# A four-layer transformer block in fp32: last token tiles reordered, one adapter product in another PSUM bank, last loads moved

## The chip, the cores and the metric

The kernel runs on one core of one Trainium2 chip. The metric is device time in microseconds of one execution of the whole program; the time before is the median of three runs. One more execution was taken with the profiler, and its trace is what the prediction reads. PE is TensorE (matmuls; PEld its weight loads), DVE is VectorE, ACT is ScalarE, POOL is GpSimd, SP is SyncE, which here issues most DMAs.

## The reference

Four stages, each followed by a residual sum and a layernorm without weights, on x of 4 batches x 1024 tokens x 1024 features, all in fp32:

```
x = layernorm(x + x @ (W0 * blockmask).T)                       # stage 0
x = layernorm(x + x @ W1.T + bias1 + lora(batch))               # stage 1: an adapter of rank 16 picked by batch
x = layernorm(x + convnet(x))                                   # 4 layers of width 128: norm, silu, long convolution, norm, MLP 512
x = layernorm(x + x @ W3.T + bias3 + sum_e routing_e lora_e(x)) # stage 3: 8 adapters of rank 16, routed by the batch's mean
```

## The kernel before, in words

**Tiles and stages.** Tokens go in eight groups of 512 (`g` = 0 to 7; a batch is two groups). Stages 0 and 1 keep features on the partitions; each is 14 products per group (a Strassen-like scheme of 7 products for 8 blocks, in two halves of the output columns, `project`, L429). Stage 3 has the tokens on the partitions: a group is two tiles of 2 x 128 tokens (`stage3(g, i, ...)`, L673), and each tile takes 7 products, k = 0 to 6, of four matmul steps with 512 columns. An fp32 matmul step is two instructions in the trace, so a product is 8 MATMULs of 512 columns, or 16 of 256 in stages 0 and 1.

**The order of the work.** One product of the main chain is one *tick*. A dictionary `plan` holds small pieces of other work by tick: `put(at, piece)` and `put_in(lo, hi, pieces, ...)` put them there, `later(n, piece)` puts one n ticks from now, and `tick()` (L373) runs what stands at the present tick and counts on. PE and DVE execute strictly in the order in which the program names their instructions (class `InOrder`: every operation of `V` and `T` is made to follow the one before, and is recorded at L104). The queues of ACT, POOL and SP are ordered by the compiler, which may issue a load as soon as its buffer is free. Ticks 28g to 28g+13 are stage 0 of group g, the 14 after them stage 1; ticks from 224 are stage 3.

**PSUM.** `bank()` gives one of four banks of 128 x 512 in the pool "mm", for the main products. `spot()` gives one of two in the pool "pc", used by `cv` (convolution result), `a_ps` (first matmul of the MLP), `aTp` (transposes of an adapter) and, in the start, two of the first products. A bank comes free when the last reader of its product (a DVE addition or an ACT copy) is done.

**Adapters.** `merge` (L731) adds an adapter to a weight matrix: for every 128 rows it multiplies two small matrices (48 rows deep in stage 1, 128 in stage 3) and DVE adds the product to the weight (`w<-w,mm`), in column halves j = 0, 1. With 48 rows the two halves lie at partitions 0 and 64 of `aT` and `b`, so the two products of a pair stand in different rows of the array. `adapt1(b)` does this for stage 1 of batch b, in 8 pieces of two products; after every second piece, `operands` makes four sums and stores the result for streaming. For batch 0 the pieces stand between the last half products of stage 0 of group 0 (`for o in range(5, KC)`, L1263); for batches 1 to 3 they are put at ticks 56b-1 to 56b+9. At tick 56b+8 three pieces and `into` (L549, the product `mm<-z,win`) come together.

**The last adapter and bias.** `last_prep` (tick 68) runs the three steps of `prep_lora(a3_d, b3_d, ...)` (L1029): load `at_raw` and `b_raw` through SP, eight transposes on PE into two spots `aTp`, copies and centring on ACT and DVE and three stores on POOL; and the same for the bias row `b3r`.

**The end of a stage 3 tile.** Rows are normed by the root of their mean square: `squares(m, n)` (ACT, with a running sum into `st`) for the column halves n of the token tiles m = 0, 1; then `spread4(m)` (a small DVE operation, a root on ACT) and `finish(m)` (reciprocal and scaling of 128 x 1024 on DVE, a store of 512 KB on SP). Product k = 5 finishes token tile 0 and k = 6 finishes token tile 1. Both `spread4` stand one tick after the tile's last product, `finish(0)` and `finish(1)` one and two ticks later still; behind the very last tile there are no products left, so they run one after the other.

Of the kernel before, what the change touches and what calls it, by code (L numbers as in the profile page):

```python
# [10 lines left out]
F32 = mybir.dt.float32  # L11
I32 = mybir.dt.int32
AF = mybir.ActivationFunctionType
ALU = mybir.AluOpType
# [3 lines left out]
P = 128  # L18
NB = 4
S = 1024  # L20
D = 1024
# [3 lines left out]
HF = 512  # L25
# [8 lines left out]
EPS = 1e-5  # L34
U = 512
NU = NB * S // U
PRODUCT = 3.7
HU = U // 2
# [15 lines left out]
def block_kernel(  # L54
# [25 lines left out]
    nc = tc.nc  # L80
    A, G = nc.scalar, nc.gpsimd
# [28 lines left out]
    V, T = InOrder(nc.vector), InOrder(nc.tensor)  # L110
    NR0 = N_LORA * R0
    NR1 = N_EXP * R1

    const = ctx.enter_context(tc.tile_pool(name="const", bufs=1))
    small = ctx.enter_context(tc.tile_pool(name="small", bufs=2))
# [63 lines left out]
    def big(name, shape, tag, bufs):  # L179
        return sb.tile(shape, F32, name=name, tag=tag, bufs=bufs)  # L180
# [7 lines left out]
    def whole(name, shape):  # L188
        return big(name, shape, "whole", 2)

    def pair(name):
        return big(name, [P, 2, D], "pair", 2)
# [4 lines left out]
    def c4(name):  # L197
        return big(name, [P, D], "c4", 2)
# [14 lines left out]
    def bank():  # L213
        return mmp.tile([P, U], F32, name="mm", tag="mm")

    def spot(name):
        return pcp.tile([P, U], F32, name=name, tag="pc")
# [73 lines left out]
    def halves(w):  # L291
        if isinstance(w, list):
            return w
        return [w[:, ds(j * HF, HF)] for j in range(2)]
# [20 lines left out]
    def product(ps, lhs, rhs, n):  # L315
        for c in range(n):
            T.matmul(ps, lhsT=lhs(c), rhs=rhs(c), start=(c == 0), stop=(c == n - 1))
        return ps
# [8 lines left out]
    def count(at, pe, dve):  # L327
        time_pe[at] = time_pe.get(at, PRODUCT) + pe
        time_dve[at] = time_dve.get(at, 0.0) + dve

    def put(at, piece, pe=0.0, dve=0.0):
        plan.setdefault(at, []).append(piece)
        count(at, pe, dve)
# [16 lines left out]
    def later(n, piece):  # L350
        put(clock[0] + n, piece)
# [321 lines left out]
    def stage3(g, i, ops, wq, bias3):  # L673

        z = whole("z4", [P, 2, D]) if g or i else pair("z4")
        (c11, c12), (c21, c22) = (halves(z[:, m, :]) for m in range(2))
        bl, br = halves(bias3)
        st = small.tile([P, 2, 2], F32, name="st4", tag="st4", bufs=4)

        def squares(m, n):  # L680
            sq = big("sq", [P, U], "sq", 2)
            A.activation(  # L682
                sq, z[:, m, ds(n * HF, HF)], AF.Square, accum_out=st[:, m, n : n + 1]
            )

        for k in range(7):
            ps = product(bank(), lambda c: ops[k][:, c, :], lambda c: wq(k, c), 4)
            if k == 0:
                V.tensor_tensor(c11, ps, bl, ALU.add)
                V.tensor_tensor(c12, ps, br, ALU.add)  # L690
            elif k == 1:
                V.tensor_tensor(c12, ps, c12, ALU.add)
                V.tensor_tensor(c21, ps, c11, ALU.add)
            elif k == 2:
                V.tensor_tensor(c12, ps, c12, ALU.add)
            elif k == 3:
                V.tensor_tensor(c22, ps, c12, ALU.add)
                squares(1, 1)
                V.tensor_tensor(c21, ps, c21, ALU.add)
            elif k == 4:  # L700
                V.tensor_tensor(c12, ps, c12, ALU.add)
                squares(0, 1)
            elif k == 5:
                V.tensor_tensor(c11, ps, c11, ALU.add)
                squares(0, 0)
            else:
                V.tensor_tensor(c21, ps, c21, ALU.add)
                squares(1, 0)
            add_squares()
            tick()  # L710

        r = small.tile([P, 2], F32, name="r4", tag="r4", bufs=3)

        def spread4(m):
            V.tensor_scalar(st[:, m, 1:2], st[:, m, 1:2], 1.0 / D, EPS, ALU.mult, ALU.add)
            A.activation(
                r[:, m : m + 1], st[:, m, 0:1], AF.Sqrt, bias=st[:, m, 1:2], scale=1.0 / D
            )

        def finish(m):  # L720
            rm = r[:, m : m + 1]
            V.reciprocal(rm, rm)
            V.tensor_scalar(z[:, m, :], z[:, m, :], rm, None, ALU.mult)
            nc.sync.dma_start(out_d[ds(g * U + (2 * i + m) * P, P), :], z[:, m, :])

        for m in range(2):
            later(0, partial(spread4, m))
            later(1 + m, partial(finish, m))


    def merge(w_of, ka, kb, n, gate, sums, q, tiles=None, keep=None):  # L731


        st = {}
        at = (0, 64) if n <= 64 else (0, 0)

        def start():
            st["a"], st["b"] = aT, b = rank("aT"), rank("b")
            for k in sorted(set(at)):
                nc.sync.dma_start(aT[ds(k, n), :], lo_s[ka][:n, :])  # L740
                nc.sync.dma_start(b[ds(k, n), :], lo_s[kb][:n, :])
                V.tensor_scalar(b[ds(k, n), :], b[ds(k, n), :], gate(k), None, ALU.mult)

        def add(c, i, js):
            if c not in st:
                if c > 1 and q is not None:
                    operands(c - 2)
                st[c] = w_of(c)
            for j in js:
                k = at[j]  # L750
                ps = product(
                    bank(), lambda _: st["a"][ds(k, n), ds((4 * i + c) * P, P)],
                    lambda _: st["b"][ds(k, n), ds(j * HF, HF)], 1,
                )
                w = halves(st[c][i])[j]
                V.tensor_tensor(w, w, ps, ALU.add)
            if i and 1 in js and q is not None:
                if c == 3 or keep:
                    operands(c)
                else:  # L760
                    put(clock[0] + 1, partial(operands, c))

        def operands(c):
            if ("done", c) in st:
                return
            st["done", c] = True
            w = st[c]
            out = tiles(c) if tiles else [half_tile("s") for _ in range(3)]
            x, y = halves(w[0]), halves(w[1])
            sums(x, y, (out[0], out[1], x[1], out[2]))  # L770
            if keep:
                keep(c, (*x, *y, *out))
            store_operands(q, (*x, *y, *out), c, nc.sync.dma_start)

        if n <= 64:
            return start, [partial(add, c, i, (0, 1)) for c in range(4) for i in range(2)]
        return start, [
            partial(add, c, i, (j,)) for c in range(4) for i in range(2) for j in range(2)
        ]

# [199 lines left out]
    for k in range(28 * NU):  # L980
        g, n = divmod(k, 28)
        stage, i = n // 14, n % 7
# [9 lines left out]
    for k in range(28 * NU, 42 * NU):  # L992
        i = (k - 28 * NU) % 7
# [35 lines left out]
    def prep_lora(a_d, b_d, ka, kb, n, queue, place):  # L1029

        st = {}

        def load():
            st["at"] = at = rank("at_raw")
            st["a"] = a = at[:, : KC * n].rearrange("p (c n) -> p c n", n=n)
            st["b"] = b = c4("b_raw")
            queue.dma_start(a, a_d)
            queue.dma_start(b[:n, :], b_d)

        def transpose():  # L1040
            st["tp"] = [place() for _ in range(2)]
            for g in range(2):
                for c in range(4):
                    T.transpose(st["tp"][g][:n, ds(c * P, P)], st["a"][:, 4 * g + c, :], ident)

        def store():
            aT, b = rank("aT"), st["b"]
            for g in range(2):
                A.copy(aT[:n, ds(g * HF, HF)], st["tp"][g][:n, :])
            G.dma_start(lo_s[ka][:n, :], aT[:n, :])  # L1050
            centre_rows(b[:n, :], D)
            G.dma_start(lo_s[kb][:n, :], b[:n, :])

        return load, transpose, store
# [208 lines left out]
    for o in range(5, KC):  # L1263
        ps = bank()
# [133 lines left out]
    ps = small.tile([P, DEPTH, NLV], F32, name="ps", bufs=1)  # L1398
# [144 lines left out]
        0.0, 1.7,  # L1543
    )

    def last_prep():
        for step in prep_lora(a3_d, b3_d, 2, 3, NR1, nc.sync, partial(spot, "aTp")):
            step()
        b3r = c4("b3r")[:1, :]
        nc.sync.dma_start(b3r, bias3_d)  # L1550
        centre_rows(b3r, D)
        G.dma_start(bias3_s, b3r)

    for n, (load, work) in enumerate([mw_prep(l) for l in range(DEPTH)] + [wout_prep()]):
        put(35 + 5 * n, load)
        put(39 + 5 * n, work)
    put(68, last_prep)
    for c in range(4):
        w3 = {}

# [21 lines left out]
    ops, rs = stage0(nxt)  # L1582
# [3 lines left out]
    for g in range(2, NU):  # L1586
        ops, rs = stage0(nxt)
# [20 lines left out]
    ops = first_x3  # L1608
    for n, (g, i) in enumerate(pairs):
        if n % 4 == 0:  # L1610
            wq = load_w3(g // 2)
        now = ops
        if n + 1 < len(pairs):
            ops = load_x3(*pairs[n + 1], clock[0] + 2)
# [61 lines left out]
```

## Time and profile before

| | |
|---|---|
| time, median of 3 runs (lowest, highest) | 1739.15 us (1738.88, 1745.45) |
| the profiled execution | 1738.38 us, span 1736.7 us |
| granted TensorE clock, mean | 0.992 |
| PE busy | 1700.5 us, 98% of the span, 6337 matmuls |
| DVE, ACT, POOL busy | 1288.7, 624.5, 210.5 us |
| DMA | 394.85 MB, mean 227 GB/s |
| product of an adapter pair, mm<-b,aT | 256 matmuls, 105.3 us busy, 7.0 us of idleness before them |
| store of a finished token tile | 32 x 512 KB, 2.7 us from issue to landing |

The span runs from the first to the last instruction. A row of a list of instructions gives start, duration, engine, line, operation, output<-inputs, shape and count, and in brackets how long the engine idled before it and what it waited for. In the list of waits, "PE mm L104 <- DVE w L104" is PE, about to write a bank of mm, held by a DVE instruction that writes w. The granted clock is a share of full speed.

### The profile page before, as it was taken

What the parts mean: (1) busy time and instruction counts of PE and PEld (TensorE: products, weight loads), DVE (VectorE), ACT (ScalarE), POOL (GpSimd) and SP (SyncE); (2) the same over time, 40 slices, a digit from 0 to 9 for tenths busy, and PEclk for the clock granted to TensorE, in tenths of its full rate; (3) what the DMA queues carried; (4) which work ended last, traced back from release to release, by engine and by line L of the source; (5) the groups of instructions that cost most, each with busy time, mean ns of one, the idle gap of its engine ahead of it and who ended that gap; (6) DMA issues with size and microseconds to landing.
All of it is one profiled execution on the core that took longest, in us unless ns stands there. A gap on an engine that the chain in (4) does not pass through costs nothing.

```text
span 1736.7 us, 19185 instructions
## 1 busy us (share of the span) xinstructions
PE 1700.5 (98%) x6337; PEld 1049.8 (60%) x6337; DVE 1288.7 (74%) x2174; ACT 624.5 (36%) x1075; POOL 210.5 (12%) x451
## 2 busy tenths in 40 slices
PE   7999999999999999999999999999999999999998
PEld 3388886677676567766765666666444444444443
DVE  5789787777567688777886797677778877676743
ACT  4411112355343235443232455323444652333011
POOL 1100110121011102201021111011201110100000
PEclk9999999999999999999999999999999999999999
DMA  9977879966745885586879656787525737964211
GB/s 356 324 242 265 281 252 351 324 205 223 267 134 164 303 294 163 160 300 210 282 262 297 225 177 225 269 264 254 187 98 198 235 125 241 364 212 146 91 67 60
DMA packets 194293, 394.85 MB, mean 227 GB/s; under 512 B 16753, under 2 KB 105985, under 8 KB 189458
## 3 DMA queue, kind: packets, MB, share of 16 engines
q1 hardware_dynamic: 188626, 375.49, 63.9%
q0 software_dynamic: 4896, 17.18, 2.6%
q8 instruction: 50, 0.82, 0.2%
q10 hardware_dynamic: 672, 0.96, 0.2%
q14 instruction: 49, 0.40, 0.1%
HBM read 267.34 MB, written 126.23 MB: 227 GB/s over the span
## 4 chain that ended last, share of the span: by engine, by line
PE 87%; DVE 8%; DMA 2%; ACT 1%; issue 1%; POOL 0%; SPq 0%; ACTq 0%; DVEq 0%; POOLq 0%
PE mm L104 71%; PE a_ps L104 6%; PE o L104 6%; PE stats L104 2%; DVE z L104 2%; PE cv L104 1%; DVE x L104 1%; DVE w L104 1%; DVE s L104 1%; DVE u L104 1%; DMA at_raw<-in_a_dram 1%; DVE tt L104 1%; DVE crs L104 1%; ACT w L221 1%; DVE ssum L104 0%
## 5 line engine op out<-in xcount | busy, mean ns | idle before, releaser
L104 DVE TENSOR_TENSOR z<-mm,z 128x512 f32<-128x512 f32 x338 | 226.2, 684 | 257.8 <-PE mm L104 256.5
L104 PE MATMUL mm<-tt,wq 128*128 128x256 f32 x1792 | 408.1, 381 | 0.0
L104 PEld LDWEIGHTS mm<-tt,wq 128*128 128x128 f32 x1792 | 337.0, 190 | 78.3 <-issue 22.2
L248 POOL PARTITION_BROADCAST crs<-sd x288 | 140.4, 597 | 869.2 <-DVE sd L104 699.7
L104 PE MATMUL mm<-w3q,x 128*128 128x512 f32 x384 | 173.0, 596 | 0.0
L104 PE MATMUL mm<-xT,wq 128*128 128x256 f32 x672 | 153.1, 382 | 0.0
L104 PE MATMUL mm<-z,wq 128*128 128x256 f32 x672 | 152.0, 380 | 0.0
L104 PEld LDWEIGHTS mm<-z,wq 128*128 128x128 f32 x672 | 127.2, 190 | 29.3 <-issue 9.4
L104 PEld LDWEIGHTS mm<-xT,wq 128*128 128x128 f32 x672 | 126.1, 190 | 26.9 <-issue 7.2
L104 PE MATMUL mm<-w3q,s 128*128 128x512 f32 x288 | 130.4, 596 | 0.0
L104 DVE TENSOR_TENSOR ssum<-ssum,sq 128x512 f32<-128x512 f32 x168 | 115.3, 687 | 14.1 <-ACT sq L387 7.3
L104 PEld LDWEIGHTS mm<-w3q,x 128*128 128x128 f32 x384 | 71.9, 190 | 88.2 <-issue 87.7
L870 ACT ACTIVATE a_sb<-a_ps,b1c 128x512 f32<-128x512 f32 x128 | 86.2, 683 | 107.7 <-PE a_ps L104 107.3
L104 PE MATMUL a_ps<-crs,mw 128*128 128x512 f32 x256 | 121.0, 595 | 3.6 <-DVE crs L104 3.6
L104 DVE RECIPROCAL sd<-sd 128x128 f32<-128x128 f32 x96 | 91.0, 948 | 42.3 <-ACT sd L242 41.0
L104 PE MATMUL o<-a_sb,mw 128*128 128x512 f32 x256 | 120.6, 592 | 0.4 <-ACT a_sb L870 0.4
L104 PE MATMUL mm<-b,aT 48*128 48x512 f32 (+1 forms) x256 | 105.3, 648 | 7.0 <-DVE z L104 4.8
L104 DVE TENSOR_TENSOR w<-w,mm 128x512 f32<-128x512 f32 x128 | 82.6, 677 | 25.0 <-PE mm L104 13.7
L682 ACT ACTIVATE sq<-z 128x512 f32<-128x512 f32 x64 | 40.2, 629 | 159.1 <-DVE z L104 146.4
L104 PEld LDWEIGHTS mm<-w3q,s 128*128 128x128 f32 x288 | 53.8, 190 | 65.4 <-issue 64.4
L242 ACT ACTIVATE sd<-stats,eps 128x128 f32<-128x128 f32 x96 | 35.2, 366 | 153.9 <-PE stats L104 106.2
L104 PEld LDWEIGHTS a_ps<-crs,mw 128*128 128x128 f32 x256 | 48.1, 190 | 57.3 <-issue 49.7
(240 smaller groups left out, 2138.6 us busy)
## 6 DMA issues: line engine op xcount, KB each, us to landing
wq<-a0q_s SPq DMA_DIRECT2D x98, 512.0 KB, 4.3
wq<-a1q_s SPq DMA_DIRECT2D x98, 512.0 KB, 4.4
w<-a_s SPq DMA_DIRECT2D x48, 512.0 KB, 5.3
w3q<-a3q_s SPq DMA_DIRECT2D x21, 1024.0 KB, 7.0
a1q_s<-w SPq DMA_DIRECT2D x64, 256.0 KB, 3.8
x_s<-z SPq DMA_DIRECT2D x16, 1024.0 KB, 5.5
x<-x_s SPq DMA_DIRECT2D x64, 256.0 KB, 5.6
x_s<-x SPq DMA_DIRECT2D x128, 128.0 KB, 2.4
```

The costliest lines, as they stand in the source:

```text
L104: ins = op(*args, **kw)
L221: A.activation(w, w, AF.Identity, accum_out=rs[: w.shape[0]])
L242: A.activation(sd[:, :seg], ps[:, :seg], AF.Sqrt, bias=eps)
L248: G.partition_broadcast(dst[:, ds(j * seg, seg)], sd[32 * j : 32 * j + 1, :seg], channels=P)
L682: A.activation(sq, z[:, m, ds(n * HF, HF)], AF.Square, accum_out=st[:, m, n : n + 1])
L870: A.activation(s, a, AF.Silu, bias=b1c[:, l * FC + f : l * FC + f + 1])
```

## The change

Three things change.

1. **Stage 3's tile ends.** In all tiles, `spread4(0)` and `finish(0)` are put one tick earlier and `spread4(1)` and `finish(1)` too, so that root and scaling of token tile 0 stand ahead of those of token tile 1. In the last tile the root of token tile 0 runs in the tick of product 5; product 6 is made in two column halves of 256, each in a bank of its own, each added and squared by itself (the second sum of squares goes to `more` and is added); token tile 0 is scaled and stored between the halves; and scaling and stores are shared: the left 512 columns are scaled by DVE and stored by SP, the right 512 by ACT and stored through ACT's queue.
2. **Adapter products.** In `merge` with 48 rows, the product for j = 1 takes a bank of the pool "pc" in place of one of "mm".
3. **The last adapter's load.** The loads of `at_raw`, `b_raw` and `b3r` are put at tick 66; transposes, copies, centring and stores at tick 70 (before: all at 68).

```
@@ stage3
+        last = (g, i) == (NU - 1, 1)
+        r = small.tile([P, 2], F32, name="r4", tag="r4", bufs=3)
+        if last:
+            more = small.tile([P, 1], F32, name="more", bufs=1)
+
-        def squares(m, n):
+        def squares(m, n, cols=slice(0, HF), out=None):
             sq = big("sq", [P, U], "sq", 2)
             A.activation(
-                sq, z[:, m, ds(n * HF, HF)], AF.Square, accum_out=st[:, m, n : n + 1]
+                sq[:, cols], z[:, m, ds(n * HF, HF)][:, cols], AF.Square,
+                accum_out=st[:, m, n : n + 1] if out is None else out,
             )
...
+        def finish(m):
+            rm = r[:, m : m + 1]
+            V.reciprocal(rm, rm)
+            out = out_d[ds(g * U + (2 * i + m) * P, P), :]
+            if last:
+                c0, c1 = halves(z[:, m, :])
+                V.tensor_scalar(c0, c0, rm, None, ALU.mult)
+                A.activation(c1, c1, AF.Identity, scale=rm)
+                nc.sync.dma_start(out[:, :HF], c0)
+                A.dma_start(out[:, HF:], c1)
+            else:
+                V.tensor_scalar(z[:, m, :], z[:, m, :], rm, None, ALU.mult)
+                nc.sync.dma_start(out, z[:, m, :])
+
+        def last_product():
+
+            for n, out in enumerate((more, None)):
+                cols = slice(n * HU, (n + 1) * HU)
+                ps = product(
+                    bank()[:, cols], lambda c: ops[6][:, c, :], lambda c: wq(6, c)[:, cols], 4
+                )
+                V.tensor_tensor(c21[:, cols], ps, c21[:, cols], ALU.add)
+                squares(1, 0, cols, out)
+                if n == 0:
+                    V.tensor_tensor(st[:, 1, 1:2], st[:, 1, 1:2], more, ALU.add)
+                    finish(0)
+            spread4(1)
+            finish(1)
+
         for k in range(7):
+            if last and k == 6:
+                last_product()
+                break
...
             elif k == 5:
                 V.tensor_tensor(c11, ps, c11, ALU.add)
                 squares(0, 0)
+                later(1 - last, partial(spread4, 0))
+                if not last:
+                    later(2, partial(finish, 0))
+                    later(2, partial(spread4, 1))
+                    later(3, partial(finish, 1))
...
-        for m in range(2):
-            later(0, partial(spread4, m))
-            later(1 + m, partial(finish, m))
@@ merge
                 ps = product(
-                    bank(), lambda _: st["a"][ds(k, n), ds((4 * i + c) * P, P)],
+                    (spot("mm") if j and n <= 64 else bank()), lambda _: st["a"][ds(k, n), ds((4 * i + c) * P, P)],
                     lambda _: st["b"][ds(k, n), ds(j * HF, HF)], 1,
                 )
@@ last_prep
+    lora3 = prep_lora(a3_d, b3_d, 2, 3, NR1, nc.sync, partial(spot, "aTp"))
+
+    def last_load():
+        lora3[0]()
+        tiles3["b"] = b3r = c4("b3r")[:1, :]
+        nc.sync.dma_start(b3r, bias3_d)
+
     def last_prep():
-        for step in prep_lora(a3_d, b3_d, 2, 3, NR1, nc.sync, partial(spot, "aTp")):
-            step()
-        b3r = c4("b3r")[:1, :]
-        nc.sync.dma_start(b3r, bias3_d)
+        lora3[1]()
+        lora3[2]()
+        b3r = tiles3["b"]
         centre_rows(b3r, D)
         G.dma_start(bias3_s, b3r)
...
-    put(68, last_prep)
+    put(66, last_load)
+    put(70, last_prep)
```

## The prediction

> **What bounds the kernel.** I read the page's busy table first (PE 1700.5 us of a span of 1736.7, 98%), then the shares of the chain that ended last, then everything that PE waits for, because with PE at 98% only PE's idle stretches and its slow stretches can be won.
>
> ```profile
> PE 87%; DVE 8%; DMA 2%; ACT 1%; issue 1%; POOL 0%; SPq 0%; ACTq 0%; DVEq 0%; POOLq 0%
> ```
>
> ```profile
> PE mm L104 <- DVE w L104: 5.2, 3, 3.1
> PE mm L104 <- DVE z L104: 4.8, 2, 2.4
> PE a_ps L104 <- DVE crs L104: 3.6, 6, 1.3
> PE aTp L104 <- DMA at_raw<-in_a_dram: 1.6, 1, 1.6
> ```
>
> The columns are total us, number of waits, and the longest. The first two rows are PE waiting for a bank that an adapter product filled and DVE has not yet emptied. The fourth is the transposes of the last adapter, waiting for their load. Together 11.6 us; with the 8 us between PE's last product (1728.9) and the end (1736.7), this is all that the change touches.
>
> Next the same waits in order of time, PE only: the start (adapter of batch 0), then batch 2.
>
> ```profile
> 59.51 1.99 PE L104 MATMUL mm<-b,aT 48*128 48x512 f32 x8
> 64.57 5.40 PE L104 MATMUL mm<-xT,w 128*128 128x512 f32 x8 [3.08 <-DVE w L104]
> ...
> 79.13 3.70 PE L104 MATMUL mm<-xT,w 128*128 128x512 f32 x8
> ```
>
> ```profile
> 587.20 1.98 PE L104 MATMUL mm<-b,aT 48*128 48x512 f32 x6
> 591.59 3.78 PE L104 MATMUL mm<-b,aT 48*128 48x512 f32 x6 [2.40 <-DVE z L104]
> 595.30 8.67 PE L104 MATMUL mm<-z,win 128*128 128x512 f32 x16
> ```
>
> The eight matmuls at 64.57 take 5.40 us where the same eight take 3.70 at 79.13. So a wait costs more than itself: the clock falls behind it. The busy table by stretches shows it (columns: us, busy us of PE, PEld, DVE, ACT, POOL, granted clock, DMA share, GB/s):
>
> ```profile
> 318.53:321.94 3.41, 1.81 (x10) 1.28 (x10) 2.68 (x4) 2.83 (x4) 1.87 (x5) 1.00 1.00 309
> 287.81:291.22 3.41, 1.92 (x8) 0.96 (x7) 3.38 (x7) 0.46 (x1) 0.00 (x0) 1.00 0.96 337
> 291.22:298.04 6.82, 6.82 (x11) 2.73 (x10) 4.16 (x7) 0.69 (x2) 0.00 (x0) 0.50 1.07 374
> 588.19:591.60 3.41, 1.00 (x5) 0.18 (x2) 3.25 (x6) 0.00 (x0) 0.09 (x1) 1.00 1.02 401
> 62.53:65.94 3.41, 1.37 (x3) 0.68 (x4) 3.28 (x7) 0.42 (x2) 1.39 (x2) 1.00 1.06 379
> ```
>
> PE ran at half clock for 6.82 us after 291.22, 591.60 and 919.28, and for 3.4 us after 65.94. The 3.41 us before each had PE busy for 1.92 (on 48 of 128 rows only), 1.00, 1.12 and 1.37 us. The transposes' wait (busy 1.81 us, most of it full products) was not followed by a fall.
>
> [...]
>
> **Part B, the second product of each adapter pair goes to the two-buffer ring "pc".** A pair (j=0, j=1) runs side by side: 1.06 us for both, 0.86 us for one alone. Work is unchanged; only the bank waits move.
>
> *Start.* Before, three free mm banks serve four products, so the next product waits for DVE's first addition (63.84 to 64.5). After, that product finds a free bank at 61.5. I follow PE with DVE's durations (additions 0.62 each, four sums 2.6, four additions to ssum 3.0): product to 65.0; group two waits for DVE's fourth addition (66.3), done 67.3; product to 70.7; group three waits for DVE's additions of group two (start 71.8 as now, second done 73.1, fourth 74.3), done 75.2; product to 78.7; group four waits for additions that start at 77.6 instead of 78.4, done 81.0; product to 84.45. Now stage 1 starts at 89.25: 4.8 us won. DVE goes along: its four tt sums now end at 96.1 and would end near 94.0, and the 2.57 us that it idles at 98.66 vanish, so the second tt sum (91.4) is there for its product (91.9). This is tight, and the new waits at 71.6 (1.5 us among 48-row products) can halve the clock for 3.4 us, price 1.7 us. I charge 1.0 and take **-3.8** (ends: -4.8, and 0 if DVE, which from 63.84 idles only twice, 0.74 and 0.41 us, holds the start of stage 1).
>
> *Batches 1 to 3.* Three pairs stand before the `win` product in one tick. In batch 2 DVE reaches the eviction of the tick's product only at 590.85, behind its own queue, and then adds until 595. Before, PE stops at the fourth product until 591.59; after, it runs five (to 590.2), and the sixth needs the bank of the second, which DVE's second addition frees at 592.75. The stop is 2.55 us instead of 2.40, later, with just as little PE work around it, so the clock falls as before. `win` starts near 594.5 instead of 595.3, but the same four or five matmuls at half clock follow. Batch 1's stop splits into 1.3 and 0.8 us. I take **0** (ends: +1 each, if the low window falls later; -3.4 each, half of 6.82, if the clock stays up).
>
> *What now shares the ring* are a_ps, cv and aTp. The narrowest places: the second a_ps product at 568.91 needs the bank that DVE's addition (567.40, 1.27 us for two) frees at 568.67; the pair at 569.86 needs the bank that ACT (569.11 + 0.69) frees at 569.80. Both hold, with 0.24 and 0.06 us to spare. Behind such a wait stands all of PE.
>
> **Part C, the last adapter's load at tick 66, its work at 70.** The wait of 1.60 goes. The load was issued on SP at 316.46, behind stores that wait for DVE's sums, and landed 5.1 us later. Even unmoved in SP's order it is there long before tick 70 (331). Behind it on SP stand streamed weights, which are five buffers ahead. b_raw and b3r load at 286.13 and 303.03 already. POOL's three stores come some 8 us later; POOL's next work is at 341.83. DVE's four centring instructions (0.13 + 0.75 + 0.13 + 0.74) leave ticks where DVE is full and go to one before which it idles 3.44 (338.35). New: at tick 70 the transposes need both pc banks behind two a_ps; ACT frees the second at 335.5, PE wants it near 335.2: 0.3. Sum **-1.3** (ends -1.6, +0.4 if both banks come late by one ACT copy each).
>
> **Part A, the end.** Now, DVE and ACT, all in line behind the last product: evict 0.69 (1728.90), square 0.63 and read 0.19, two roots 0.46, reciprocal 0.16, scale 0.75, reciprocal, scale 0.75, to 1732.43.
>
> ```profile
> 1728.90 0.69 DVE L104 TENSOR_TENSOR z<-mm,z 128x512 f32<-128x512 f32 x1 [2.74 <-PE mm L104]
> ...
> 1731.68 0.75 DVE L104 TENSOR_SCALAR z<-z,r 128x1024 f32<-128x1024 f32 x1
> ```
>
> Two stores of 512 KB go out at 1731.6 and 1732.5; bytes move from 1732.4 to 1735.0 at about 400 GB/s; the span ends 1.65 later. After: two column halves of 16 shorter matmuls take as long as eight (3.4 to 3.6 in both forms). The first half is evicted near 1727.2, squared by 1728.15; then tile 0's reciprocal, scale of one half on DVE (0.48, row of a 128x512 TENSOR_SCALAR) and of the other on ACT (0.63), and its stores near 1729. The second half is evicted by 1729.35 (0.4, between 0.69 and the 0.35 of half the columns). Its square waits on ACT behind tile 0's scale and store issue (0.41 to 0.46 on ACT's queue), until 1729.6; root 1730.4, reciprocal 1730.6, scales 1731.1 and 1731.3, stores issued there. Then 0.8 to the first byte and 1.3 us for 512 KB: 1733.2 instead of 1735.0, **-1.8** (ends: -0.8 if ACT's scale and issue run 1 us later, -2.4 if the halves go out in 0.65 us).
>
> In the other 15 tiles root and scale come a tick earlier and apart. At most a table load more per tile (1.28 us, seven in 16 tiles now) falls on ACT, which is busy 36%: 0.
>
> **Sum.** -3.8 + 0 - 1.3 - 1.8 = -6.9. The profiled execution took 1738.38 us (span 1736.7 and 1.7 around it), 0.77 under the median of the runs: 1731.5 by the profile, **1732** against the median of 1739.15. About 0.5%, or 8.7 us, is what a measurement can tell from no change; the bound is 1730.45.
>
> **Rivals.**
> - *The clock stays up in batches 1 to 3* (0.15). For: the rearranged stops fall closer to full products, and 53% busy was enough at 318.53. Against: 2.55 us of idleness between 48-row products is more than the 2.04 that sufficed at 62.53. Two to three times 3.4 less: 1722 to 1725. [...]
> - *The start gives nothing* (0.22): DVE, or a halved clock among the new waits, holds stage 1 near 89. Then only A and C remain: 1739.15 - 3.1 = 1736.
> - *Slower* (0.07): the pc ring blocks a_ps. If DVE's addition at 568 comes over 1.7 us later than now (0.24 to spare plus 1.5 of stop), the clock falls there: 1.5 + 3.4 us at two places in each of batches 2 and 3, 19.6 in all: 1751.
> - The forecast itself (0.56): 1728.5 to 1735.5.
>
> Faster by over 0.5%: the first rival and a fifth of the forecast, 0.27. Slower: 0.07. The rest, 0.66, within. Range 1726 to 1738: it leaves out most of the first rival and the slower one.
>
> **What would show it.** Start: no wait at 61.5, stage 1's first product near 85 (mm<-z,w, now 89.25). Batches: stops of 1.3 to 2.6 us and half clock still there; if 1.00 throughout, the first rival. C: no wait at aTp, at most 0.3 behind ACT. End: the last store issued near 1.2 us earlier from PE's last product. Wrong would be any new PE wait of a_ps or cv for DVE w.

## The result and the profile after

The kernel after the change took **1734.81 us** (median of 13 runs, 1733.58 to 1735.62), the kernel before, in 13 runs beside it, 1739.15 us (1737.54 to 1745.45). The ratio is 0.9969, with a 95% interval of 0.9961 to 0.9977: 4.3 us faster, 0.31%, which is within the 0.5% that the prediction counted as no change. 1732 was forecast, so 2.8 us of the 7.15 that were expected did not come.

The profiled execution after took 1735.62 us, span 1733.9. That is the slowest of its 13 runs, while that of before lay 0.77 us under its median: the two traces are 2.8 us apart and the medians 4.3. The traces say where time went; the medians say how much there is in all. Some executions have a granted clock of 0.988 to 0.990, against 0.991 or more in the others, and most of these take longer (of the 25 runs of the kernel before beside experiments 5 to 8, six with 0.989 took 1744.0 to 1745.7 us, those with 0.991 or more 1737.1 to 1740.6), so a median also depends on how many of them it holds.

What PE waits for after the change (columns: total us, number of waits, the longest):

```profile
PE mm L104 <- DVE w L104: 7.7, 4, 2.8
...
PE mm L104 <- DVE ssum L104: 2.0, 1, 2.0
...
PE stats L104 <- DVE qe L104: 0.9, 1, 0.9
...
PE aTp L104 <- ACT a_sb L901: 0.2, 1, 0.2
```

The two rows of adapter products (DVE w 5.2 and DVE z 4.8 before) have become one of 7.7. The 1.6 us of the transposes are 0.2. And there are two rows that no line of the prediction has: ssum, 2.0, and qe, 0.9. (A third new row, 0.5 us behind ACT's csq near 751 us, is part of what drifts between batches 2 and 3 in the table below.)

**Where the time went.** The same matmuls can be laid side by side in both traces. The difference of their start times (after minus before) changes only at a few places:

| place | difference runs from .. to | worth, us | predicted |
|---|---|---|---|
| first loads, to 21 us | 0 .. -0.93 | -0.9 | - |
| adapter of batch 0, 59 to 86 | -0.93 .. -4.01 | -3.1 | -3.8 |
| batch 1, near 290 | -4.01 .. -4.52 | -0.5 | 0 |
| transposes of the last adapter, near 330 | -4.52 .. -5.47 | -1.0 | -1.3 |
| batches 2 and 3, with what drifts between them | -5.47 .. -5.06 | +0.4 | 0 |
| wout product at 1524.35 | -5.06 .. -1.79 | **+3.3** | 0 |
| routing sums at 1583.22 | -1.79 .. -0.98 | **+0.8** | 0 |
| behind PE's last product | -0.98 .. -2.8 | -1.8 | -1.8 |

The first row is no part of the change: the same difference is +0.01 in the trace of one experiment below and -1.06 in that of another.

*The start*, PE alone:

```profile
60.49 3.70 PE L104 MATMUL mm<-xT,w 128*128 128x512 f32 x8
...
72.21 2.32 PE L104 MATMUL mm<-b,aT 48*128 48x512 f32 x6 [0.96 <-DVE w L104]
74.46 5.40 PE L104 MATMUL mm<-xT,w 128*128 128x512 f32 x8
...
85.24 7.07 PE L104 MATMUL mm<-z,w 128*128 128x256 f32 x32
```

The stop of 3.08 us ahead of the first product is gone (60.49, no bracket), stage 1 begins at 85.24 instead of 89.25, and the fall of the clock has moved to the product at 74.46: 5.40 us for eight matmuls that take 3.70 at 60.49, with the granted clock at 0.50 from 74.53 to 77.94.

*Batch 2*, PE alone, and the stretches around the falls (columns: us, busy us of PE, PEld, DVE, ACT, POOL, granted clock, DMA share, GB/s):

```profile
581.74 2.84 PE L104 MATMUL mm<-b,aT 48*128 48x512 f32 x10
587.33 2.07 PE L104 MATMUL mm<-b,aT 48*128 48x512 f32 x2 [2.75 <-DVE w L104]
589.33 9.12 PE L104 MATMUL mm<-z,win 128*128 128x512 f32 x16
```

```profile
71.11:74.53 3.42, 2.39 (x8) 0.67 (x7) 3.35 (x6) 0.82 (x2) 0.00 (x0) 1.00 1.04 340
...
1521.79:1525.20 3.41, 1.42 (x4) 0.49 (x3) 1.89 (x3) 0.72 (x2) 0.00 (x0) 1.00 0.91 264
1525.20:1528.61 3.41, 3.41 (x5) 1.35 (x4) 1.89 (x3) 0.72 (x1) 0.00 (x0) 0.50 1.05 384
```

Ten matmuls of adapter pairs now go through where six did, then comes the stop, 2.75 us, and 6.83 us of half clock from 586.53, as before. The first row of the second list is the stretch ahead of the fall in the start. The last two are new: a stretch with PE busy for 1.42 us, and 3.41 us of half clock behind it, at a place where before had none.

*The end*, behind PE's last product (1727.90):

```profile
1727.94 0.42 DVE L104 TENSOR_TENSOR z<-mm,z 128x256 f32<-128x256 f32 x1
...
1729.72 0.72 ACT L705 ACTIVATE z<-z,r 128x512 f32<-128x512 f32 x1 [0.23 <-DVE r L104]
1729.72 0.49 DVE L104 TENSOR_SCALAR z<-z,r 128x512 f32<-128x512 f32 x1
1730.47 0.37 ACTq L707 DMA_DIRECT2D out_dram<-z  x1
```

DVE and ACT scale a half each from 1729.72 on; the scaling is done 2.5 us behind PE's last product (before: 3.6), and the span ends 6.0 us behind it (before: 7.8).

**The new loss.** The stop that the waits put down to ssum, PE first, then SP's queue, after:

```profile
1518.77 3.60 PE L104 MATMUL mm<-w3q,x 128*128 128x512 f32 x8
1524.35 1.22 PE L104 MATMUL mm<-h,wout 128*128 128x512 f32 x2 [1.99 <-DVE ssum L104]
```

```profile
1513.74 0.35 SPq L710 DMA_DIRECT2D out_dram<-z  x1
1514.14 2.02 SPq L579 DMA_DIRECT2D x<-x_s  x3
1517.71 0.34 SPq L710 DMA_DIRECT2D out_dram<-z  x1
1518.96 0.33 SPq L572 DMA_DIRECT2D wout<-wout_s  x1
1519.34 1.24 SPq L579 DMA_DIRECT2D x<-x_s  x2
1520.69 5.31 SPq L964 DMA_DIRECT2D w<-a_s  x8
```

And before the change, PE at the same product, then SP's queue:

```profile
1527.84 1.10 PE L104 MATMUL mm<-h,wout 128*128 128x512 f32 x2 [0.42 <-DMA wout<-wout_s]
```

```profile
1507.74 6.80 SPq L579 DMA_DIRECT2D x<-x_s  x4
1522.77 0.34 SPq L724 DMA_DIRECT2D out_dram<-z  x1
1524.02 0.33 SPq L572 DMA_DIRECT2D wout<-wout_s  x1
1526.08 0.34 SPq L724 DMA_DIRECT2D out_dram<-z  x1
1526.52 4.18 SPq L933 DMA_DIRECT2D w<-a_s  x8
```

In both kernels PE wants `wout` 3.4 us after its load is issued (1522.36 and 1527.42), and a store of a finished tile goes out 1.25 us ahead of that load. Before, the load landed in 3.7 us; after, in 5.3. What changed is the order on SP. Before, five loads of `x` (256 KB each) went out from 1506.3 to 1514.5, ahead of both stores of the tile, and behind `wout` stood the tile's second store, which waited for DVE's scaling until 1526.08. Since the change the tile's first store stands ahead of the same five loads, and SP stood still in front of it from 1502.0 to 1513.74. So the last two of them went out 0.4 and 1.0 us behind `wout`.

The DMA packets in the traces show what that does. `wout` and the stores move in packets of 4 KB, `x` in packets of 1 KB, and the eight loads `w` for the next adapter in packets of 2 KB. After the change, the packets of `x` begin 2.8 us behind the issue of `wout` and run among the last third of its own: from 1521.70 to 1523.50 there are 268 packets of 1 KB, 43 of 4 KB and none of 2 KB. The last packet of `wout` starts 4.7 us behind the issue (if the packets of 4 KB are taken in the order of issue); before, where no packet of 1 KB runs beside it, 3.0 us. The eight loads `w` are not what slows it: their first packet comes 4.6 us behind the issue of `wout` after and 4.3 before. That it is the two loads of `x` is read from the packets; no run takes them away by themselves.

DVE is named because its instruction (ssum, to 1524.29) ended next to the landing (1524.27); it is not what PE needed, as experiments 4, 6 and 7 show.

### The profile page after: what moved, and what is told of

Read it like the earlier page. It is cut to its first block, busy times and chain, and to the rows that moved or that the text cites. A ratio compares the mean times of both kernels' runs of the same rounds, so it can differ in the third digit from the quotient of the medians.

```text
span 1733.9 us, 19205 instructions
## 1 busy us (share of the span) xinstructions
PE 1700.6 (98%) x6345; PEld 1050.1 (61%) x6345; DVE 1287.4 (74%) x2176; ACT 635.3 (37%) x1085; POOL 210.9 (12%) x451
## 4 chain that ended last, share of the span: by engine, by line
PE 85%; DVE 8%; DMA 3%; ACT 2%; issue 1%; POOL 0%; SPq 0%; ACTq 0%; DVEq 0%; POOLq 0%
PE mm L104 70%; PE a_ps L104 6%; PE o L104 6%; PE stats L104 2%; DVE z L104 2%; PE cv L104 1%; DVE w L104 1%; DVE x L104 1%; DVE u L104 1%; DVE tt L104 1%; DVE crs L104 1%; DMA w<-a_s 1%; DVE s L104 1%; DVE ssum L104 1%; ACT w L221 0%
## 5 line engine op out<-in xcount | busy, mean ns | idle before, releaser
L687 ACT ACTIVATE sq<-z 128x512 f32<-128x512 f32 (+1 forms) x65 | 40.4, 622 | 159.8 <-DVE z L104 135.9
```

Source lines behind the costliest of these rows:

```text
L687: A.activation(sq[:, cols], z[:, m, ds(n * HF, HF)][:, cols], AF.Square, accum_out=st[:, m, n : n + 1] if out is None else out,)
```

## The experiments

My theory: the three parts that were reckoned are worth about what was reckoned, and the earlier scaling in the other 15 tiles, reckoned at nothing, takes back 3 to 4 us through SP's queue and the clock behind it. Rivals: the bank costs more than it shows, or the traces merely differ from run to run. Beside each median stands that of the kernel before on the same chip: 1739.56 us (23 runs) for the first four, 1739.26 us (25 runs) for the others.

### 1. The changed kernel with the other 15 tiles ended as before

```
@@ stage3, from the kernel after
             elif k == 5:
...
-                later(1 - last, partial(spread4, 0))
-                if not last:
-                    later(2, partial(finish, 0))
-                    later(2, partial(spread4, 1))
-                    later(3, partial(finish, 1))
+                if last:
+                    later(0, partial(spread4, 0))
...
             tick()
+        if not last:
+            for m in range(2):
+                later(0, partial(spread4, m))
+                later(1 + m, partial(finish, m))
```

> The changed kernel, but in the 15 other tiles of stage 3 root and scaling stand where they stood before; the last tile, the bank and the load stay changed. Theory: the stop of 1.99 us at 1524 in the changed kernel, the 3.4 us of half clock after it and the 0.8 us at 1583 come from the earlier scaling, which lets SP issue nine loads sooner, beside the load of wout. Then this run has no half clock near 1525, wout lands in about 3.7 us instead of 5.3, and the time is 3 to 4 us less than the changed kernel: 1731. Rival: the stop comes from the other parts having moved everything by 5 us against the transfers; then it stays, and the time is 1734 to 1735.

Measured: 1731.76 us (1730.78 to 1733.37, 6 runs), ratio 0.9945 (0.9928 to 0.9962). That is the time that was forecast for the whole change. SP's queue and PE in its trace:

```profile
1519.86 0.33 SPq L572 DMA_DIRECT2D wout<-wout_s  x1
1521.91 0.34 SPq L710 DMA_DIRECT2D out_dram<-z  x1
1522.36 4.53 SPq L965 DMA_DIRECT2D w<-a_s  x8
```

```profile
1523.56 1.10 PE L104 MATMUL mm<-h,wout 128*128 128x512 f32 x2 [0.30 <-DMA wout<-wout_s]
```

The store is back behind `wout`, the five loads of `x` are ahead of both stores again (out by 1511.1), the load lands in 3.6 us, the stop is 0.30 us, and no slow stretch follows it (the next eight matmuls, from 1524.50, take 3.60 us, as eight do at 1519.66). Against the trace of after, PE gains 3.4 us at these products and 0.8 us at the routing sums; the medians, each taken against the kernel before beside it, differ by 3.5. So the prediction's error lies in the ends of the other 15 tiles. The expectation counted nine loads beside `wout`; by the packets it is two.

### 2, 3. The bank alone; the last adapter's load alone

```
@@ merge, from the kernel before
-                    bank(), lambda _: st["a"][ds(k, n), ds((4 * i + c) * P, P)],
+                    (spot("mm") if j and n <= 64 else bank()), lambda _: st["a"][ds(k, n), ds((4 * i + c) * P, P)],
```

> The kernel before with the second product of each 48-row adapter pair in the pool pc, nothing else. Theory: only the start gains, 3 to 4 us on PE (stage 1 begins near 85 to 86 instead of 89); in batches 1 to 3 the clock still falls for 6.8 us each. Time 1735 to 1736. Rival: part of the start's gain is given back before stage 3 because DVE holds PE later; then 1737 to 1739. Second rival: the batches gain too, then 1731 or less.

Measured: 1735.67 us (1732.23 to 1739.41, 12 runs), ratio 0.9973 (0.996 to 0.9985). The start gave 3.1 us in its trace as in the whole change. At the transposes the wait grew from 1.6 to 2.4 us: PE comes earlier, the load does not, so 0.8 us went back.

For the third, the two `put` lines and `last_load` of part 3 of the change were put into the kernel before:

> The kernel before with the last adapter's load at tick 66 and its work at tick 70, nothing else. Theory: the wait of 1.6 us at the transposes becomes one of 0.2 to 0.3 behind ACT, gain 1.0 to 1.4 us: 1738. Rival: the load only changes place and another wait takes it: 1739.

Measured: 1737.43 us (1736.1 to 1741.26, 12 runs), ratio 0.9981 (0.9969 to 0.9994). In the trace PE gains 1.06 us at the transposes, whose wait is 0.2 us behind ACT; the medians are 2.1 us apart, and what the rest of that is was not found.

### 4. The long product ahead of the adapter pairs

Batches 1 to 3 lose most in one tick: three pieces, each an adapter pair, then `into`. In batch 2 of after PE makes ten of the pairs' twelve matmuls in 2.84 us and then stops for 2.75, while DVE is busy for 3.38 of the 3.41 us from 583.11 on; behind them stand 7 us of full products (sixteen matmuls, 7.03 us in experiment 8). Here `into` goes first.

```
@@ leave, from the kernel after
-        later(8 if g < NU - 1 else 7, into)
+        plan.setdefault(clock[0] + (8 if g < NU - 1 else 7), []).insert(0, into)
```

> The changed kernel, but in the tick where three adapter pieces and the product with win come together, win goes first, so that DVE has 6.9 us to clear its queue before PE needs the adapter banks. Theory: in batches 1 to 3 PE loses some 6.4 us each in that tick (16.6 us for 10.1 us of work), by a stop of 2 to 2.5 us and then 6.8 us at half clock. With win first the stop and the half clock go: 15 to 19 us less than the changed kernel, 1716 to 1720, and granted clock 1.00 from 80 to 1500. Rival: DVE is the bound there and the stop only moves behind win, into the next tick: 1730 to 1735.

Measured: 1732.45 us (1730.71 to 1734.3, 6 runs), ratio 0.9948 (0.993 to 0.9965): far from what was expected. In batches 2 and 3 PE gained 6.0 and 5.9 us at that tick against the trace of after, of which 1.0 and 0.8 went back at the next matmuls into `a_ps` (their waits for DVE's crs grew). The mean granted clock of its runs is 0.994 to 0.995, that of after 0.991 to 0.993. Batch 1 lost 7.0, PE first, then SP:

```profile
307.76 2.07 PE L104 MATMUL mm<-b,aT 48*128 48x512 f32 x2 [8.77 <-DVE w L104]
```

```profile
301.89 0.81 SPq L815 DMA_DIRECT2D w<-a_s  x2
```

The weights of the last pair are loaded into buffers that come free only when the sums before them are stored. With `into` ahead, DVE's sums and their stores come later, the load is issued at 301.89, DVE stood idle for 10.4 us before the addition that uses it, and PE stood behind DVE. Behind the stop PE was slow: two matmuls of a pair took 2.07 us, against 1.12 at 297.88, and the sixteen of the next product 5.53, against 3.72 at 293.37. (This kernel, too, has the early scaling, and in its trace the stop at the `wout` product, 2.3 us, bears the name of the load and not of DVE.)

### 5, 6. The end of the last tile alone; all tile ends alone

Both are the kernel before with part 1 of the change: the fifth with the other 15 tiles left as they were (the edit of experiment 1), the sixth with them changed too.

> The kernel before with the last tile's end alone: product 6 in two column halves, scaling and stores shared; the other tiles, the bank and the load as before. Theory: 1.8 us less behind PE's last product and nothing else: about 1737.5 against 1739.2 to 1739.6 for the kernel before. Rival: the halves delay each other on ACT, 0.8 us or less.

> The kernel before with all of the tile ends changed (last tile, and root and scaling a tick earlier in the 15 others), bank and load as before. Theory: the earlier scaling costs 3 to 4 us at 1524 to 1584 by itself, whatever the shift, so the ends together lose 1.5 to 2.5 us: 1741, with a stop at mm<-h,wout and half clock after it near 1530. Rival: the collision needs the shift of 5 us by the other parts; then 1737.5 as for the last tile alone.

Measured: the last tile alone 1736.87 us (1734.49 to 1743.54, 12 runs), ratio 0.9983 (0.9969 to 0.9998); all tile ends 1741.88 us (1738.0 to 1748.96, 12 runs), ratio 1.0016 (1.0 to 1.0032). So the other 15 tiles cost 5.0 us between these two medians, on a kernel that has neither the bank nor the moved load; among the runs with a granted clock above 0.990 alone the medians are 1739.93 and 1736.64, 3.3 us apart. The cost needs neither the bank nor the moved load. In the trace of the sixth the wout load lands in 5.0 us, and this time the wait bears its name:

```profile
PE mm L104 <- DMA wout<-wout_s: 1.7, 1, 1.7
```

The wait for qe is 0.9 us, as in after. At these two places that trace loses 1.3 and 0.8 us; the half clock that was expected behind the first did not come (two matmuls in 1.02 us at 1537.42). What else the difference holds stays open. The profiled run itself (span 1744.4, clock 0.990) is a poor witness for the sum: ten matmuls from 72.79 on take 8.1 us, against 4.8 from 72.53 on in before, and sixteen from 271.74 on take 6.75, against 3.70 at 278.46; it loses 3.4 us at each of these places, which no tile end touches.

### 7. The changed kernel without the load

If the load is what PE waits for, taking it away must cure the stop, whatever DVE does with ssum. The last group takes the copy of `wout` that the group before it has loaded.

```
@@ leave, from the kernel after
-                st["w"] = c4("wout")
-                nc.sync.dma_start(st["w"], wout_s)
+                if g == NU - 1:
+                    st["w"] = kept_wout[0]
+                else:
+                    st["w"] = c4("wout")
+                    nc.sync.dma_start(st["w"], wout_s)
+                    kept_wout[:] = [st["w"]]
```

> The changed kernel, but the last group's product with wout uses the copy of wout that the group before it loaded, so that the load of 512 KB which the stop waits for does not exist. Theory: the stop of 1.99 us at mm<-h,wout and the 3.4 us of half clock go (3.3 to 3.7 us); the 0.9 us at stats<-qe stays, for it waits for DVE: 1731.5. Rival: the stop waits for DVE, as its row says (DVE ssum); then it stays and the time is 1734.8.

Measured: 1733.03 us (1730.93 to 1734.47, 8 runs), ratio 0.9956 (0.994 to 0.9972). PE in its trace:

```profile
1517.94 3.60 PE L104 MATMUL mm<-w3q,x 128*128 128x512 f32 x8
1521.37 1.02 PE L104 MATMUL mm<-h,wout 128*128 128x512 f32 x2
```

No stop, no slow stretch behind it (the next eight matmuls, from 1522.23, take 3.60 us), 3.9 us won at this place against the trace of after. The work of DVE is unchanged, and here its ssum runs from 1522.78, when the product has long begun: it never held PE. By medians the gain is 1.8 us, not 3.3, and the intervals of the two ratios overlap; the profiled run is the fastest of the eight, and how much of the 3.9 us the others win is not shown. The 0.9 us at the routing sums are still there, as they must be: they have another cause. DVE in the same trace:

```profile
1576.12 0.75 DVE L104 TENSOR_SCALAR z<-z,r 128x1024 f32<-128x1024 f32 x1
...
1578.05 0.27 DVE L104 TENSOR_REDUCE qe<-qr 128x8 f32<-128x64 f32 x1
```

This is the second scaling of the tile; the first stands at 1574.01, so both are ahead of qe. In experiment 1 one of the two, with its reciprocal, stands behind it (1579.89, qe at 1579.51): 0.15 + 0.75 us, the 0.9 that PE waits.

### 8. What the findings make together

Experiment 1 (the other tiles as before), the kept `wout`, and `into` first in batches 2 and 3 alone:

```
@@ leave, from experiment 1 with the edit of experiment 7
-        later(8 if g < NU - 1 else 7, into)
+        if g in (3, 5):
+            plan.setdefault(clock[0] + 8, []).insert(0, into)
+        else:
+            later(8 if g < NU - 1 else 7, into)
```

> The changed kernel with the other tiles' ends as before, wout kept as in the run above, and the product with win ahead of the adapter pieces in batches 2 and 3 only; in batch 1 the order stays, because there a weight's load came too late behind it (a wait of 8.8 us in the run with win first in all three). Theory: two times 5.3 to 6.0 us less than the run with the other tiles' ends as before: 1731.8 - 11.4 - 0.3 = 1720, and no half clock after 300. Rival: with the stops gone, weights streamed by DMA come too late somewhere after 600: 1724 to 1730.

Measured: **1722.73 us** (1721.02 to 1723.35, 5 runs), ratio 0.9898 (0.9878 to 0.9917), 9.0 us under experiment 1 and faster than both kernels, but 2.7 us more than the theory said. PE at the start and in batch 2:

```profile
75.75 3.70 PE L104 MATMUL mm<-xT,w 128*128 128x512 f32 x8
...
84.93 7.07 PE L104 MATMUL mm<-z,w 128*128 128x256 f32 x32
```

```profile
583.12 7.03 PE L104 MATMUL mm<-z,win 128*128 128x512 f32 x16
590.08 3.62 PE L104 MATMUL mm<-b,aT 48*128 48x512 f32 x12
```

In batch 2 neither a stop nor half clock is left: the granted clock is 1.00 from 587.60 to 594.42; while PE makes `win`, DVE clears its queue (it is idle from 587.60 to 591.01), and the twelve matmuls of the pairs then pass. At the start this run happened to keep its clock (3.70 at 75.75), with a stop ahead of it of 0.97 us where after has 0.96. The mean granted clock of its runs is 0.996 to 0.997. Against the trace of experiment 1, batches 2 and 3 win 5.8 us each in that tick, but 3.7 and 4.7 in all: PE now comes to the next matmuls into `a_ps` before DVE is ready, and their wait for its crs grows from 0.2 to 2.1 us in batch 2 and to 1.2 in batch 3. The rival, weights that come too late, is not in its list of waits.

## Why the prediction was right or wrong, point by point

- **Failed: "In the other 15 tiles root and scale come a tick earlier and apart. ... 0."** The step counted what falls on ACT and stopped there. It cost 4.1 us in the trace of after (3.3 + 0.8), 3.05 between the medians of after and experiment 1, and 3.3 to 5.0 between the sixth and the fifth. That covers the error of 2.8 us. What it left out is what the scaling carries with it: a store of 512 KB in SP's order, which now holds back loads of `x` until two of them run beside `wout`, and 0.9 us of DVE ahead of qe. The traces show it at two places only. One of them could have been found: a wait of 0.4 us for `wout` stood in the list of before, so that load had nothing to spare. Nor is it true, then, that the adapter waits, the transposes and the end were all that the change touched.
- **The start, -3.8: measured -3.1, and the step that was mis-sized is the 1.0 charged for the clock.** The walk through DVE's additions put stage 1 at 84.45 without a fall. Experiment 8 had no fall: 84.93 in its trace, 84.56 when the 0.37 us by which its first matmuls came later than before's are taken off. With the fall it costs the 1.7 us that was given as its price, and 4.8 - 1.7 is 3.1. A cost of all or nothing was entered at a value between, which neither case has.
- **Batches 1 to 3, 0: right.** The stop in batch 2 was reckoned at 2.55 us and is 2.75, five products pass ahead of it as reckoned, and the half clock stayed. In batch 1 the first of the two stops that were reckoned is there (1.25 us for 1.3), the second (0.8) is not. That the sum of the three places is about nothing holds; that they could not be won does not, as experiment 8 shows.
- **The rival in which the clock stays up: fallen** for this change. In the trace of after each of the three batches has its 6.83 us of half clock (from 286.16, 586.53 and 914.21), behind stretches of 3.41 us in which PE was busy for 2.17, 1.47 and 1.89. The two other falls came behind stretches with 1.42 (from 1521.79) and 2.39 (from 71.11).
- **The last adapter, -1.3: measured -1.0**, by itself -1.06 in its trace. The wait behind ACT, allowed at 0.3, is 0.2.
- **The end, -1.8: measured -1.8** in the trace and 2.4 by itself between medians. From PE's last product on, the reckoned times hold to 0.15 us: the second half evicted after 0.45 us (measured 0.46), root ended after 1.5 (1.6), the scalings after 2.2 and 2.4 (2.3 and 2.5).
- **The slower rival, the ring blocking a_ps: did not happen.** Its row is 3.6, 6 waits, in before and after. The 0.24 us that the trace of before left it were enough.
- **The sum.** The three parts that were reckoned, each alone, gave -3.9, -2.1 and -2.4 by medians, -8.4 together; in one kernel (experiment 1) they gave -7.8. The forecast of -6.9 would have been good for that kernel, but each part by itself gave more between its medians than at its own place in its trace (3.1, 1.06 and 1.8), so that agreement is worth no more than the spread of the runs.

## What to carry to other kernels

A step that is moved takes its DMAs with it, and on a queue kept in order a store that waits for something also holds back whatever stands behind it (here SP stood still from 1502.0 to 1513.74, ahead of a store with five loads behind it): before moving it, read in the queue's own list which loads it will then stand ahead of, and which load with no slack will then have to share the DMA engines with them (here `wout`, 5.3 us to landing instead of 3.7). A wait that the profile puts down to an engine that had other business there is tested by taking the suspected load away. And where small products outrun the engine that empties their banks, putting a long product ahead of them in the same tick can be worth more than another bank (in batch 2 these products took 10.5 us in experiment 8, against 16.6 in after with the other bank alone), as long as the loads of their operands do not hang on that very engine.

## What the runs showed of the hardware that was not expected

- **The falls had two lengths.** In the traces of before and after each of the nine falls between the first product and PE's last lasts 3.41 us (at 65.94 before, at 74.53 and 1525.20 after) or 6.83 (at 291.22, 591.60 and 919.28 before, at 286.16, 586.53 and 914.21 after). The times at full clock between them (221.87, 293.55 and 320.85 us before; 208.21, 293.55, 320.85 and 604.16 after) are whole multiples of half of 6.827 us: 65, 86 and 94; 61, 86, 94 and 177.
- **The same stop was worth different amounts.** The stop of 2.75 us in batch 2 is the same in after and in experiment 2. The eighteen matmuls behind it took 11.1 us in the one (stop from 584.6 to 587.3, granted clock 0.50 from 586.53) and 9.8 in the other (586.3 to 589.1, 0.50 from 589.94).
- **How busy PE is did not settle it.** In after the clock fell behind stretches of 3.41 us with PE busy for 2.39 (from 71.11) and 2.17 (from 282.75), where PE had 48-row products around the stop; behind the stretch at 318.53 of the kernel before, with 1.81, mostly full products, it stayed at 1.00 (321.94 to 325.35). What else decides was not shown.
- **The load of `wout` took longer with two loads close behind it on its queue:** 512 KB of `wout` took 3.6 to 3.7 us from issue to landing with only a store issued in the 2.5 us behind it (before, experiment 1), and 5.0 to 5.3 us with two loads of 256 KB, in packets of 1 KB, issued 0.4 and 1.0 us behind it (after, experiment 6).
